# An LSTM step on Trainium2: the output gate in the bank of the other gates, and h Wh partly in 512 columns

## The chip, the cores and the metric

The kernel runs on one core of one Trainium2 chip. The metric is the device time of one launch in microseconds, as the median of three runs, and lower is better. The engines have the names of the profile: PE is TensorE (matrix products; PEld its weight loads), DVE is VectorE, ACT is ScalarE, POOL is GpSimd, SP issues transfers. Each runs its own instructions in order and waits for the others by semaphores. PSUM is the memory that TensorE writes its products to; this kernel uses all of its eight banks, each 512 fp32 columns wide.

## The reference

One LSTM layer over 512 steps, with a batch of 32 and 512 units, added to its input. Everything is fp32.

```python
xW = jnp.einsum('ntd,dg->ntg', x, Wx) + b
def step(carry, xw_t):
    prev_h, prev_c = carry
    a = xw_t + prev_h @ Wh
    i = sigmoid(a[:, :Hd]); f = sigmoid(a[:, Hd:2*Hd])
    o = sigmoid(a[:, 2*Hd:3*Hd]); g = tanh(a[:, 3*Hd:])
    next_c = f * prev_c + i * g
    next_h = o * tanh(next_c)
    return (next_h, next_c), next_h
out = x + swapaxes(scan(step, (h0, 0), swapaxes(xW, 0, 1)), 0, 1)
```

`prev_h @ Wh` needs the step before and so cannot be batched: it is 32 x 512 by 512 x 2048 in each step. `x @ Wx` needs no step and can be done ahead.

## The kernel before

**One step of the recurrence.** The gates lie in PSUM as 128 partitions by 512 columns: partition block j (32 partitions) holds the batch for units 128j to 128j+127, and the columns are four gates of 128 units, put in the order i, f, g, o by the host's layout of the weights. A step k is one call of `h_part` (L766), one `cell` (L797) and, between them, other work of TensorE, all written in the loop at L1065. `h_part` multiplies: for each of four row blocks k of Wh and each of four unit blocks j one matmul (L770) with a 32-column stationary block of h. The four j run side by side in four column strips of the array. In the profile an fp32 matmul is two records, so a step's 32 matmuls are 64 records.

**Two banks by turns, and where the output gate lies.** There are two gate banks, `gates[0]` and `gates[1]`. Step t has its gates i, f and g (columns 0 to 383, `IFG`) in `gates[t % 2]`, and its output gate (columns 384 to 511) in the other bank, `gates[(t + 1) % 2]`. So `h_part` runs sixteen matmuls of 384 columns into one bank, then sixteen of 128 columns into the other.

**Seeds.** Before TensorE adds h Wh, ScalarE copies the finished x Wx of that step into the bank: `seed_first(k + 2)` (L751, copy at L755) the first 384 columns of step k+2, `seed_last(k + 1)` (L757, copy at L761) the last 128 columns of step k+1, which lie in the same bank. Both stand in the program right behind the cell of step k. The matmuls accumulate onto the seed (`start=False`).

**The cell** (L797 to L817): on ScalarE the sigmoid of i and f (L807), the tanh of g (L808), the sigmoid of o (L809); on VectorE f c (L810), i g (L811), their sum c (L812); on ScalarE tanh c (L813); on VectorE the product with o (L814) and a transpose in 32 x 32 blocks (L815), which gives `ht`, the h that the next `h_part` loads as weights. GpSimd then adds x to h and SP stores it (L873, L876).

**The other work.** x Wx is computed some steps ahead by a fast scheme for matrix products that needs 26 block products in place of 32. Each of them is a job of seven products, and a product is four matmuls of 256 columns (L477). A job starts in its own window, the one of step k having the number v = k + 4, and its products are spread over the windows up to four later; `products(v)` (L486) issues those of a window behind `h_part`. From v = `START` on the jobs repeat with a cycle of `PER` = 32 windows, 26 jobs or 182 products to a cycle, so a window holds five or six. In the head, before `START`, a job sums over two factors and a window can hold up to fourteen. `evacuate(v)` (L495), which stands between `h_part` and `products`, moves the finished sums between PSUM and SBUF on ScalarE and VectorE, and `run_due` (L362) gives VectorE the sums for later jobs; all of these stand ahead of the cell in the two engines' queues. The results go to HBM and come back by `load_xw` on GpSimd's queue three steps ahead of their use.

**The end.** The last 40 steps use another form, `h_halves` (L779), which the change leaves as it is.

Of the kernel before, what the change touches and what calls it, by code (L numbers as in the profile page):

```python
# [14 lines left out]
P = 128  # L15
B = 32
T = 512
NJ = 4
G = 4
IFG = 3 * P  # L20
# [16 lines left out]
PER = ROW * MO  # L37
# [107 lines left out]
def windows_of(k):  # L145

    return [k + 4]


START = windows_of(HEAD - LEAD)[0]  # L150
# [4 lines left out]
def begin(n):  # L155

    half, at = divmod(n, R // 2)
    return PER // 2 * half + at + (at >= 5) + (at >= 9)
# [7 lines left out]
LAST = START + PER * (NSB - 1) + begin(R - 1)  # L166
HALVES = LAST + 3 - 4
# [14 lines left out]
def kernel(  # L182
# [9 lines left out]
    nc = tc.nc  # L192
# [11 lines left out]
    gates = [psum.tile([P, G * P], F32, name=f"gates_{i}") for i in range(2)]  # L204
# [13 lines left out]
    rows, xw, stored = {}, {}, {}  # L218
# [233 lines left out]
    jobs = {}  # L452
    count = 0

    def new_job(w, late5=False):
        nonlocal count
        job = Job()
        job.w, job.w5 = w, w + late5
        job.acc = accs[w % 2][:, w // 2 % 2]
        job.pp = pps[2 * count % 3], pps[(2 * count + 1) % 3]  # L460
        count += 1
        jobs[w] = job
        return job

    def product(job, s):
        dst = {
            1: job.acc,
            6: job.acc,
            7: job.acc,
            5: p5[:, 0],  # L470
            2: job.pp[0][:, 0],
            3: job.pp[0][:, 1],
            4: job.pp[1][:, 0],
        }[s]
        for m, (a, w) in enumerate(job.factors(s)):
            for t in range(4):
                nc.tensor.matmul(  # L477
                    dst[t * B : (t + 1) * B],
                    a[:, t],
                    w,  # L480
                    start=s in (1, 5) and m == 0,
                    stop=True,
                    skip_group_check=True,
                )

    def products(v):  # L486
        for late, ss in ((4, (4,)), (2, (7,)), (0, (1,)), (1, (6,)), (0, (5,)), (1, (5,)), (3, (2, 3))):
            job = jobs.get(v - late)
            for s in ss if job else ():
                if s != 5 or job.w5 == v:  # L490
                    product(job, s)
                if s == 4:
                    job.release()
# [207 lines left out]
    whole, given = [], [0, 0]  # L701
# [45 lines left out]
    def seed_half(t, m):  # L747
        if t < T:
            nc.scalar.copy(bank_half(m), half(xw[t], m))

    def seed_first(t):  # L751
        if t == HALVES:
            seed_half(t, 0)
        elif t < HALVES:
            nc.scalar.copy(gates[t % 2][:, 0:IFG], xw[t][:, 0:IFG])  # L755

    def seed_last(t):  # L757
        if t == HALVES:
            seed_half(t, 1)
        elif t < HALVES:  # L760
            nc.scalar.copy(gates[(t + 1) % 2][:, IFG:], xw[t][:, IFG:])  # L761

    state = {"c": c_init, "ht": h_init}
    ig = work.tile([P, P], F32, name="ig")

    def h_part(t):  # L766
        for g, cols in ((gates[t % 2], slice(0, IFG)), (gates[(t + 1) % 2], slice(IFG, G * P))):
            for k in range(NJ):
                for j in range(NJ):
                    nc.tensor.matmul(  # L770
                        g[j * B : (j + 1) * B, cols],
                        state["ht"][:, k, :],
                        wh_sb[:, k, j, cols],
                        start=False,
                        stop=True,
                        skip_group_check=True,
                    )
# [19 lines left out]
    def cell(t):  # L797
        n, tt = divmod(t, ROW)
        s = work.tile([P, G, P], F32, name=f"s_{t}", tag="s")
        fc = work.tile([P, P], F32, name=f"fc_{t}", tag="fc")  # L800
        c = work.tile([P, P], F32, name=f"c_{t}", tag="c", bufs=2)
        tc_t, h = ig, fc
        ht = work.tile([P, NJ, B], F32, name=f"ht_{t}", tag="ht", bufs=3)

        g = gates[t % 2].rearrange("p (g u) -> p g u", u=P)
        o = gates[(t + 1) % 2].rearrange("p (g u) -> p g u", u=P)[:, 3]
        nc.scalar.activation(s[:, 0:2], g[:, 0:2], AF.Sigmoid)  # L807
        nc.scalar.activation(s[:, 2], g[:, 2], AF.Tanh)  # L808
        nc.scalar.activation(s[:, 3], o, AF.Sigmoid)  # L809
        nc.vector.tensor_mul(fc, s[:, 1], state["c"])  # L810
        nc.vector.tensor_mul(ig, s[:, 0], s[:, 2])  # L811
        nc.vector.tensor_add(c, fc, ig)  # L812
        nc.scalar.activation(tc_t, c, AF.Tanh)  # L813
        nc.vector.tensor_mul(h, s[:, 3], tc_t)  # L814
        nc.vector.transpose(ht.rearrange("p q b -> p (q b)"), h)  # L815
        state["c"], state["ht"] = c, ht
        put_step(t)  # L817
# [50 lines left out]
    def put_step(t):  # L868
        n, tt = divmod(t, ROW)
        ht = state["ht"]  # L870
        if tt % 2 == 0:
            state["oc"] = opool.tile([P, 2, NJ, B], F32, name=f"oc_{t}", tag="oc")
        (nc.gpsimd if t < T - 3 else nc.vector).tensor_add(state["oc"][:, tt % 2], xr[t][:, tt % 2], ht)  # L873
        if tt % 2 == 1 or t == T - 2:
            m = tt % 2 + 1
            nc.sync.dma_start(  # L876
                out=out[n][:, (tt + 1 - m) * P : (tt + 1) * P],
                in_=state["oc"][:, 0:m].rearrange("p t q b -> p (t q b)"),
            )
# [3 lines left out]
    for u, (i, j) in zip(UNIT_AT, UNITS):  # L883
        job = new_job(u)
        job.kind = (i, j)
    for sb in range(NSB):
        for n in range(R):
            job = new_job(START + PER * sb + begin(n), n % (R // 2) in (4, 8, 12))
            job.kind = (sb, n)
    for w, j in zip(LATE_AT, LATE_ORDER):  # L890
        job = new_job(w)
# [125 lines left out]
    with tc.manual_schedule():  # L1017
# [23 lines left out]
        for op in prepare(0):  # L1041
            op()
        products(0)
        for t in range(1, 4):
            keep_direct(t, firsts[t])
# [4 lines left out]
        for v, t in enumerate(range(4, ROW), 1):  # L1050
            direct(t, gates[t % 2])
            for op in prepare(v):
                op()
            if v < 4:
                evacuate(v, 0)
            run_due(0, 2400 if v > 1 else 0)
            keep_direct(t, gates[t % 2])
            if v < 4:
                products(v)
                fetch(v)  # L1060
        seed_first(0)
        seed_last(0)
        seed_first(1)

        for k in range(T):  # L1065
            if k % 2 == 0 and k + 2 < T:
                load_residual(k + 2)
            if 2 * 4 - 3 <= k and k + 3 < LATE_END:
                load_xw(k + 3)
            (h_part if k < HALVES else h_halves)(k)  # L1070
            for m, v in enumerate(windows_of(k)):
                if v == START + 4:
                    assert len(due) == 0 or due[0][0] >= START
                    head_done()
                announce(v)
                room = HEAD_ROOM if v < START - 4 else ROOM if k < HALVES - 1 else HALF_ROOM
                run_due(v, room - evacuate(v, room))
                products(v)
                tail_products(v)
                fetch(v)  # L1080
                if k == T - 2:
                    x_last()
                if 2 * 4 - 4 <= k and k + 4 < LATE_END:
                    fill_bias(k + 4)
                if m == 0:
                    (cell if k < HALVES else cell_halves)(k)
                    seed_first(k + 2)
                    seed_last(k + 1)
                for op in prepare(v + 1):
                    op()  # L1090
# [52 lines left out]
```

## Time and profile before

| | us |
|---|---|
| median of three runs | 3089.14 (3089.09 to 3089.30) |
| the profiled execution | 3089.44 |
| its span, first to last instruction | 3087.6 |
| TensorE with a matmul in flight | 3077.6 |
| VectorE busy | 2247.7 |
| ScalarE busy | 1972.5 |

The page of the profile lists busy times by engine, the chain of work that ended last, and groups of instructions by source line; the timeline lists instructions by start time, with the idle time of the engine just before them and what ended it in brackets. A matmul's recorded duration includes its way through the array, so those of neighbours overlap; the distance from start to start is what a matmul costs in a stream.

### The profile page before, as it was taken

How to read it: one execution, taken by the hardware profiler on the slowest of the kernel's cores; microseconds unless marked ns; L12 is line 12 of the kernel's file. 1: busy time of each engine (PE TensorE's matmuls, PEld its weight loads, DVE VectorE, ACT ScalarE, POOL GpSimd, SP SyncE). 2: the span in 40 equal slices, each digit the busy share in tenths (PEclk: the TensorE clock that was granted, in tenths of full speed). 3: DMA queues.
4: the chain of work that ended last, by engine and by line, in shares of the span. 5: the costliest groups of instructions: out<-in, count | busy, mean ns of one | idle time of the engine just before them, and what ended most of it. 6: DMA issues, size and time to landing. Idle time of an engine off the chain costs nothing.

```text
span 3087.6 us, 133855 instructions
## 1 busy us (share of the span) xinstructions
PE 3077.6 (100%) x56756; PEld 2216.0 (72%) x56756; DVE 2247.7 (73%) x6345; ACT 1972.5 (64%) x5694; POOL 807.4 (26%) x1009
## 2 busy tenths in 40 slices
PE   9999999999999999999999999999999999999998
PEld 6777666666666666666666666677777777777766
DVE  6735777777777777777777777777777777777654
ACT  2556666666666666666666666766666666666654
POOL 0112222222222222222222222222222222222321
PEclk9999999999999999999999999999999999999999
DMA  8857898988989888898888988889898898887752
GB/s 281 260 149 191 222 261 216 261 226 225 260 216 254 223 241 238 216 265 217 253 228 217 265 221 250 225 220 261 216 260 224 227 255 222 253 229 222 188 114 45
DMA packets 345973, 696.14 MB, mean 225 GB/s; under 512 B 45216, under 2 KB 118176, under 8 KB 344864
## 3 DMA queue, kind: packets, MB, share of 16 engines
q1 hardware_dynamic: 273520, 557.27, 55.1%
q0 software_dynamic: 71424, 130.06, 26.8%
q8 instruction: 446, 7.31, 1.0%
q14 instruction: 151, 1.24, 0.1%
q10 hardware_dynamic: 432, 0.27, 0.0%
HBM read 503.65 MB, written 183.76 MB: 223 GB/s over the span
## 4 chain that ended last, share of the span: by engine, by line
PE 99%; DVE 1%; ACT 0%; DMA 0%; issue 0%; DVEq 0%
PE gates L770 53%; PE acc L477 17%; PE pp L477 17%; PE p L477 6%; PE gates L784 4%; PE gates L682 1%; PE pp L682 1%; PE acc L682 0%; PE pp L1021 0%; DMA xw<-t 0%; DVE fc L835 0%; DVE c L837 0%; DVE t L656 0%; DVE fc L841 0%; DVE ht L845 0%
## 5 line engine op out<-in xcount | busy, mean ns | idle before, releaser
L770 PE MATMUL gates<-wh_sb,ht 128*32 128x384 f32 (+1 forms) x30144 | 1759.3, 379 | 0.0
L770 PEld LDWEIGHTS gates<-wh_sb,ht 128*32 128x32 f32 x30144 | 1188.4, 110 | 551.9 <-issue 439.7
L873 POOL TENSOR_TENSOR oc<-xr,ht 128x128 f32<-128x128 f32 x509 | 385.5, 757 | 2243.1 <-DVE ht L815 2037.3
L732 POOL DMA_DIRECT2D xw<-xw x496 | 437.1, 881 | 20.4 <-issue 2.1
L807 ACT ACTIVATE s<-gates 128x256 f32<-128x256 f32 x472 | 182.0, 386 | 351.9 <-PE gates L770 341.6
L477 PE MATMUL pp<-wb,nodes 128*32 128x256 f32 x3808 | 342.4, 379 | 0.0
L728 ACT COPY xw<-bias_sb 128x512 f32<-128x512 f32 x496 | 314.0, 633 | 0.0
L810 DVE TENSOR_TENSOR fc<-s,c 128x128 f32<-128x128 f32 x471 | 136.6, 290 | 208.2 <-ACT s L807 205.2
L814 DVE TENSOR_TENSOR fc<-s,ig 128x128 f32<-128x128 f32 x472 | 137.9, 292 | 177.2 <-ACT ig L813 177.2
L516 ACT COPY pp<-pu 128x512 f32<-128x512 f32 x388 | 234.0, 603 | 50.2 <-DVE t L640 23.7
L518 DVE TENSOR_TENSOR pp<-acc,p 128x256 f32<-128x256 f32 x388 | 165.9, 427 | 137.1 <-ACT pp L517 137.1
L477 PE MATMUL pp<-wb,s 128*32 128x256 f32 x2576 | 231.2, 379 | 0.0
L477 PE MATMUL acc<-wa,s 128*32 128x256 f32 x2576 | 230.8, 379 | 0.0
L477 PE MATMUL acc<-wb,s 128*32 128x256 f32 x2576 | 230.7, 379 | 0.0
L477 PE MATMUL p<-wa,s 128*32 128x256 f32 x2576 | 230.6, 379 | 0.0
L809 ACT ACTIVATE s<-gates 128x128 f32<-128x128 f32 x472 | 131.1, 278 | 147.3 <-PE gates L770 147.3
L755 ACT COPY gates<-xw 128x384 f32<-128x384 f32 x468 | 221.2, 473 | 3.3 <-DVE nodes L698 3.0
L813 ACT ACTIVATE ig<-c 128x128 f32<-128x128 f32 x472 | 146.2, 310 | 101.5 <-DVE c L812 63.8
L511 DVE TENSOR_TENSOR pu<-acc,p 128x256 f32<-128x256 f32 x388 | 161.4, 416 | 46.0 <-ACT p L508 35.4
L517 ACT COPY pp<-acc 128x256 f32<-128x256 f32 x388 | 140.0, 361 | 83.0 <-DVE t L640 41.0
L477 PEld LDWEIGHTS pp<-wb,nodes 128*32 128x32 f32 x3808 | 167.4, 110 | 23.7
L815 DVE STREAM_TRANSPOSE ht<-fc 128x128 f32<-128x128 f32 x472 | 147.2, 312 | 50.3 <-DVE fc L814 1.4
(241 smaller groups left out, 4751.9 us busy)
## 6 DMA issues: line engine op xcount, KB each, us to landing
wb<-keep_b SPq DMA_DIRECT2D x322, 512.0 KB, 6.3
xw<-xw POOLq DMA_DIRECT2D x496, 256.0 KB, 5.6
wa<-keep_a SPq DMA_DIRECT2D x322, 384.0 KB, 5.2
xw<-t SPq DMA_DIRECT2D x408, 128.0 KB, 3.9
xw<-raw_sb SPq DMA_DIRECT2D x312, 128.0 KB, 4.0
xr<-in_x_dram SPq DMA_DIRECT2D x256, 128.0 KB, 5.5
out_dram<-oc SPq DMA_DIRECT2D x255, 128.0 KB, 4.4
row<-in_x_dram SPq DMA_DIRECT2D x63, 512.0 KB, 8.2
```

Source lines behind the costliest of these rows:

```text
L477: nc.tensor.matmul(dst[t * B : (t + 1) * B], a[:, t], w, start=s in (1, 5) and m == 0, stop=True, skip_group_check=True,)
L511: nc.vector.tensor_add(job.pu[:, 1], job.acc, job.p5)
L516: nc.scalar.copy(job.pp[0], job.pu)
L518: nc.vector.tensor_add(job.pp[1][:, 1], job.acc, job.p5)
L728: nc.scalar.copy(xw[t], bias_sb)
L732: nc.gpsimd.dma_start(out=xw[t], in_=stored[i][a], accum_op=mybir.AluOpType.add)
L755: nc.scalar.copy(gates[t % 2][:, 0:IFG], xw[t][:, 0:IFG])
L770: nc.tensor.matmul(g[j * B : (j + 1) * B, cols], state["ht"][:, k, :], wh_sb[:, k, j, cols], start=False, stop=True, skip_group_check=True,)
L807: nc.scalar.activation(s[:, 0:2], g[:, 0:2], AF.Sigmoid)
L813: nc.scalar.activation(tc_t, c, AF.Tanh)
L815: nc.vector.transpose(ht.rearrange("p q b -> p (q b)"), h)
L873: (nc.gpsimd if t < T - 3 else nc.vector).tensor_add(state["oc"][:, tt % 2], xr[t][:, tt % 2], ht)
```

## The change

The output gate of step t goes back to `gates[t % 2]`, beside i, f and g; `seed_first` copies all 512 columns at once and `seed_last` does nothing but for the last form. `h_part` multiplies its first `whole` row blocks of Wh in matmuls of 512 columns, and the other row blocks as before, first their 384 and then their 128 columns, all into the one bank. `whole` is three at 13 positions of the cycle of 32, two at three positions, one at one position, and none at the others. In the head it is four, that is all, in windows with more than seven products (`products_at` counts them) and none in the others. In the changed file the cell starts at L825 (L825, L826 and L827 are the three activations on ScalarE, L828 is the product f c on VectorE), the tanh of c is L831, the transpose L833, and the matmul of `h_part` is L788.

```diff
         elif t < HALVES:
-            nc.scalar.copy(gates[t % 2][:, 0:IFG], xw[t][:, 0:IFG])
+            nc.scalar.copy(gates[t % 2], xw[t])
...
         if t == HALVES:
             seed_half(t, 1)
-        elif t < HALVES:
-            nc.scalar.copy(gates[(t + 1) % 2][:, IFG:], xw[t][:, IFG:])
...
+    WIDE = {at: 3 for at in (0, 3, 10, 15, 16, 17, 19, 20, 21, 22, 26, 28, 31)} | {5: 2, 6: 1, 23: 2, 27: 2}
+
     def h_part(t):
-        for g, cols in ((gates[t % 2], slice(0, IFG)), (gates[(t + 1) % 2], slice(IFG, G * P))):
-            for k in range(NJ):
+        v = t + 4
+        if v < START:
+            whole = NJ if products_at(v) > 7 else 0
+        else:
+            whole = WIDE.get((v - START) % PER, 0) if v < LAST else 0
+        first, last = slice(0, IFG), slice(IFG, G * P)
+        parts = [(slice(0, G * P), range(whole))] + [(cols, range(whole, NJ)) for cols in (first, last)]
+        for cols, ks in parts:
+            for k in ks:
                 for j in range(NJ):
                     nc.tensor.matmul(
-                        g[j * B : (j + 1) * B, cols],
+                        gates[t % 2][j * B : (j + 1) * B, cols],
                         state["ht"][:, k, :],
                         wh_sb[:, k, j, cols],
                         start=False,
...
-        o = gates[(t + 1) % 2].rearrange("p (g u) -> p g u", u=P)[:, 3]
+        o = g[:, 3]
         nc.scalar.activation(s[:, 0:2], g[:, 0:2], AF.Sigmoid)
         nc.scalar.activation(s[:, 2], g[:, 2], AF.Tanh)
         nc.scalar.activation(s[:, 3], o, AF.Sigmoid)
```

```python
IN_ORDER = ((4, (4,)), (2, (7,)), (0, (1,)), (1, (6,)), (0, (5,)), (1, (5,)), (3, (2, 3)))

def products_at(v):
    found = 0
    for late, ss in IN_ORDER:
        job = jobs.get(v - late)
        for s in ss if job else ():
            if s != 5 or job.w5 == v:
                found += 1 if job.w >= START else 2
    return found
```

More of the change, by code (lines that the diff above doesn't have):

```diff
@@ L484, in product @@
                 )
+    IN_ORDER = ((4, (4,)), (2, (7,)), (0, (1,)), (1, (6,)), (0, (5,)), (1, (5,)), (3, (2, 3)))
+    def products_at(v):
+        found = 0
+        for late, ss in IN_ORDER:
+            job = jobs.get(v - late)
+            for s in ss if job else ():
+                if s != 5 or job.w5 == v:
+                    found += 1 if job.w >= START else 2
+        return found
     def products(v):
-        for late, ss in ((4, (4,)), (2, (7,)), (0, (1,)), (1, (6,)), (0, (5,)), (1, (5,)), (3, (2, 3))):
+        for late, ss in IN_ORDER:
             job = jobs.get(v - late)
```

## The prediction

> **What bounds the kernel now.** I read the page first, then the waits of TensorE, then the timeline of a few steps in the middle of the run. The page says that TensorE sets the end:
>
> ```profile
> span 3087.6 us, 133855 instructions
> PE 3077.6 (100%) x56756; PEld 2216.0 (72%) x56756; DVE 2247.7 (73%) x6345; ACT 1972.5 (64%) x5694; POOL 807.4 (26%) x1009
> ...
> PE 99%; DVE 1%; ACT 0%; DMA 0%; issue 0%; DVEq 0%
> ```
>
> Only 10 us of the span are without a matmul, and the view of the waits has TensorE waiting for another engine six times in all:
>
> ```profile
> PE gates L784 <- DVE fc L835: 4.0, 5, 1.2
> PE pp L1021 <- DVE c_init L249: 1.1, 1, 1.1
> ```
>
> None of them is in the 472 steps of L770, so today the recurrence is hidden in every step. How closely it is hidden is read from the timeline. Three steps in a row, TensorE alone (a row is start, time to its last modelled end, line; eight records of L477 are one product of the other work):
>
> ```profile
> 615.06 3.67 PE L770 MATMUL gates<-wh_sb,ht 128*32 128x384 f32 x64
> ...
> 621.11 3.67 PE L770 MATMUL gates<-wh_sb,ht 128*32 128x384 f32 x64
> 624.56 0.65 PE L477 MATMUL pp<-wb,row 128*32 128x256 f32 x8
> 624.99 0.65 PE L477 MATMUL acc<-wb,s 128*32 128x256 f32 x8
> ...
> 626.72 3.67 PE L770 MATMUL gates<-wh_sb,ht 128*32 128x384 f32 x64
> ```
>
> A step is h Wh (3.45 us, 621.11 to 624.56) and then products of 0.43 us each (624.56 to 624.99). The step at 615.06 has six products and takes 6.05 us; the one at 621.11 has five and takes 5.61. Beside them runs the cell of the same step, here for the step that begins at 626.72 (call that moment H0) and ends at 632.76, 6.04 us later:
>
> ```profile
> 629.60 0.38 ACT L807 ACTIVATE s<-gates 128x256 f32<-128x256 f32 x1 [0.89 <-PE gates L770]
> 629.88 0.27 ACT L808 ACTIVATE s<-gates 128x128 f32<-128x128 f32 x1
> 630.02 0.29 DVE L810 TENSOR_TENSOR fc<-s,c 128x128 f32<-128x128 f32 x1 [0.27 <-ACT s L807]
> ...
> 630.48 0.28 ACT L809 ACTIVATE s<-gates 128x128 f32<-128x128 f32 x1 [0.32 <-PE gates L770]
> 630.55 0.29 DVE L812 TENSOR_TENSOR c<-fc,ig 128x128 f32<-128x128 f32 x1
> ...
> 630.87 0.31 ACT L813 ACTIVATE ig<-c 128x128 f32<-128x128 f32 x1
> ...
> 631.09 0.47 ACT L755 COPY gates<-xw 128x384 f32<-128x384 f32 x1
> 631.21 0.29 DVE L814 TENSOR_TENSOR fc<-s,ig 128x128 f32<-128x128 f32 x1 [0.38 <-ACT ig L813]
> ...
> 631.59 0.27 ACT L761 COPY gates<-xw 128x128 f32<-128x128 f32 x1
> 631.61 0.31 DVE L815 STREAM_TRANSPOSE ht<-fc 128x128 f32<-128x128 f32 x1
> ...
> 632.76 0.87 PE L770 MATMUL gates<-wh_sb,ht 128*32 128x384 f32 x8
> ```
>
> Three times matter. The first sigmoid (L807) starts 2.88 us after H0, when the sixteen 384-column matmuls are through. The output gate's sigmoid (L809) starts 3.76 us after H0, when the sixteen 128-column ones are through. From L807 to the end of the transpose (631.92) the cell takes 2.32 us, and L809 is not on that path: its result is first wanted by L814. So h stands ready 0.84 us before TensorE wants it in a six-product step, and 0.43 us less than that in a five-product step. The present order lives on one overlap: 0.88 us of the cell run while TensorE still writes the output gate into the other bank.
>
> **The change part by part.**
>
> *Output gate into the same bank.* In the changed program's instruction order the first sigmoid (L825) waits for TensorE and the output gate's (L827) has no wait of its own; before, L807 and L809 each had one. TensorE's semaphore is now raised once per step, at the last matmul of h Wh, by all its 20 or 32 at a time, where it was raised by 16 and again by 16. So the first sigmoid can start only when the output gate's columns are done too, that is when L809 starts today: 3.76 us after H0. The split into 384 and 128 columns that remains in the code then frees nothing early. From there the cell needs its 2.32 us (the output sigmoid now follows L826 at once and is ready some 0.8 us into the cell, before the tanh of c has even begun at 1.27). Then h goes to TensorE. That hand-over is seen as a real wait only at the end of the run:
>
> ```profile
> 3068.99 0.24 DVE L845 STREAM_TRANSPOSE ht<-fc 128x64 f32<-128x64 f32 x1
> ...
> 3069.38 1.50 PE L784 MATMUL gates<-wh_sb,ht 128*32 128x256 f32 x24 [1.17 <-DVE fc L835]
> ```
>
> It is 0.15 us from the transpose's end (3069.23). From above it is bounded by the tightest kind of step that does not stall, where the next block began 0.27 us after the transpose ended:
>
> ```profile
> 696.93 0.31 DVE L815 STREAM_TRANSPOSE ht<-fc 128x128 f32<-128x128 f32 x1
> ...
> 697.51 3.67 PE L770 MATMUL gates<-wh_sb,ht 128*32 128x384 f32 x64
> ```
>
> I take 0.15, since there TensorE truly waited, for the same kind of tile. A step can then be no shorter than S = 3.76 + 2.32 + 0.15 = 6.23 us (6.35 with the upper bound), whatever its products: TensorE ends its six products at 6.04, its five at 5.61, and waits. Of the 472 steps 311 have six products and 139 five, counted in the program's order; 22, all at the start, have seven or more (7 x 0.43 + 3.45 = 6.46) and stay hidden. The added stall is 311 x 0.19 = 59.1 us and 139 x 0.62 = 86.2 us.
>
> The Trainium skill, "PSUM — Partial Sum Buffer", section "PSUM bank collisions raise a hardware error", says that TensorE writing and ScalarE reading one bank in the same 32 partitions at once is an error even at different columns, so a semaphore has to guard the whole bank. By that rule the wait of L825 for the last matmul is not an accident of the build, and the sum is the one above; by the rows alone, in which L807 runs beside L770, one could count on keeping the overlap, and the sum would be that of the second rival. No run here shows a collision.
>
> *Merged columns.* What a merged block saves is bounded by a block that is in 512 columns already, the direct x Wx of the first rows:
>
> ```profile
> 22.03 3.65 PE L682 MATMUL gates<-raw_sb,row 128*32 128x512 f32 x32
> ```
>
> That is eight groups of four records in 3.65 us, against 3.67 for the eight of 384 and eight of 128: 0.02 us in eight groups, 2.5 ns for each group merged. Three row blocks are six groups (15 ns). The program merges three blocks in 179 stalled steps, two in 42, one in 14 (1270 groups), and 148 groups in hidden steps of the start: 1418 x 2.5 ns = 3.5 us in all.
>
> *Seeds.* L755 and L761 (0.47 and 0.27) become one copy of 512 columns. The nearest row of that size into a bank is
>
> ```profile
> L516 ACT COPY pp<-pu 128x512 f32<-128x512 f32 x388 | 234.0, 603 | 50.2 <-DVE t L640 23.7
> ```
>
> 0.60 us, so ScalarE saves 0.14 us per step. It stands behind the tanh of the cell and seeds a step that is two further on; the cover is the whole next step, and I cost it at nothing.
>
> *Behind the later wait.* On ScalarE the seed and the next step's evacuation copies queue behind L825. The seed would end 3.76 + 1.49 (L755 after L807) + 0.60 = 5.85 us after H0, 0.38 before the next block; the copies then wait for TensorE anyway, as in this row, which starts 0.31 us after the block at 632.76:
>
> ```profile
> 633.07 0.59 ACT L628 COPY raw_sb<-pp 128x512 f32<-128x512 f32 x1 [1.20 <-PE pp L477]
> ```
>
> On VectorE the next sums start 0.15 us before the next block and not 0.84. There the cover is thinner: it is the first rival.
>
> *Sum.* 59.1 + 86.2 - 3.5 = +141.8 us. On the span: 3087.6 + 141.8 = 3229.4; around it lie 1.8 us (profiled execution 3089.44), and the median of the runs is 0.3 lower, 3089.14. That gives 3231.
>
> **The rivals.**
>
> *VectorE falls behind.* In some steps VectorE is not ready when the first sigmoid is:
>
> ```profile
> DVE fc L810 <- ACT s L807: 205.2, 270, 5.2
> ...
> 618.78 0.29 DVE L810 TENSOR_TENSOR fc<-s,c 128x128 f32<-128x128 f32 x1
> ...
> 1013.15 0.43 DVE L518 TENSOR_TENSOR pp<-acc,p 128x256 f32<-128x256 f32 x1 [1.57 <-ACT pp L517]
> ```
>
> L810 waits for ScalarE in 270 of 471 steps; in the step of 615.06 it starts 3.72 us after H0 where the clean step has 3.30. In the changed kernel it is wanted at 3.76 + 0.42 = 4.18, so 0.46 is to spare. If all of VectorE's work moved by the 0.69 that it starts later, it would be 0.23 late, and 201 such steps cost 46 us more: 3277. Against it: this lateness comes from work like L518, which sits waiting (1.57 us) for a copy that waits for TensorE, and so keeps its distance to H0. It decides from 4.18 us after H0.
>
> *The first gates are released by their columns.* If L825 were freed by the last 384-column matmul, the overlap stays. With three blocks merged those matmuls end six groups of about 0.11 us later, 0.64, inside the 0.84 of the six-product steps, and the other steps keep their order. Then only the merging is left: 3089.1 - 3.5 = 3085.6, 0.11% less, not told from no change. For it: the profile has L807 and L809 released separately. Against it: the changed program has a single wait and a single raise, at the end of the block. It decides at where L825 starts, 3.5 or 3.74 us after H0 in a merged step and 2.88 or 3.76 in an unmerged one.
>
> **How the numbers follow.** I give the forecast 0.87, VectorE behind 0.07, release by columns 0.03, and 0.03 to something else. For the forecast alone, each row that is read to 0.01 us can move 450 steps by 4.5 us either way, some 15 us for the few that make up S and the steps' lengths, and a hand-over of 0.27 would add 54 us. Below, nothing shortens a chain whose parts are all measured, so the range goes 16 us down, and up by a little over half of the 54: 3215 to 3262. It leaves out the two rivals' own values and little of the forecast. A measurement of this kernel tells 0.2% (6.2 us) from no change. Slower by more than that: forecast, VectorE and most of the rest, 0.96; within it, 0.03; faster, 0.01.
>
> **What would show it.** After the change the waits of TensorE should have a new row, the h block waiting for VectorE's transpose, some 450 times and about 145 us in all; L825 should start about 3.75 us after the block's first matmul in every step, L827 should show no wait for TensorE; steps of five and six products should be of one length, 6.21 to 6.23 us. TensorE's busy time should hardly change. L825 starting 2.9 us after H0 would make the first part wrong; steps of 6.4 us with L828 (the new place of L810) not waiting for the sigmoid would speak for VectorE; a hand-over above 0.2 us would make the price too small.

## The result and the profile after

The changed kernel takes 3173.77 us (3173.62 to 3173.95) against 3089.16: slower by 84.6 us, ratio 1.0274 with a 95% interval of 1.0261 to 1.0287. That it would be slower was forecast; the loss of 141.8 us was too large, and 3173.8 lies below the range that began at 3215.

The page of the changed kernel:

```profile
span 3172.1 us, 121564 instructions
PE 3121.8 (98%) x51084; PEld 1583.7 (50%) x51084; DVE 2244.1 (71%) x6345; ACT 1830.3 (58%) x5222; POOL 807.1 (25%) x1009
...
PE 88%; DVE 7%; ACT 3%; issue 1%; DMA 0%; DVEq 0%
```

The last row is the chain that ended last, by engine: it was 99% TensorE and now runs through VectorE and ScalarE for a tenth of the time. The work of TensorE did not grow (fewer, wider records), yet its busy time rose by 44 us. A matmul's recorded time includes its way through the array: eight records of L477 last 0.61 us while the next eight start after 0.43, so the beginning of each wait still counts as busy. For the same reason the view of the waits shows only a part of the stall at the matmuls: in a step of six products the last record ends after the next block has begun (644.02 + 0.61 = 644.63 against 644.49 in the rows below), and no wait is left to see. The weight loads, which read h, tell the number of waits:

```profile
PEld gates L788 <- DVE ht L833: 212.1, 450, 0.8
...
PE gates L788 <- DVE ht L833: 40.0, 142, 0.3
```

450 waits for the transpose is the forecast number of stalled steps, 311 + 139. The timeline of TensorE, two block starts in a row (the step from 626.19 has six products, the one from 632.29 five; the second row shows only the beginning of its block):

```profile
626.19 3.66 PE L788 MATMUL gates<-wh_sb,ht 128*32 128x384 f32 x64
632.29 2.14 PE L788 MATMUL gates<-wh_sb,ht 128*32 128x384 f32 x24
```

and the next block, at 638.40, with its whole cell (all engines, some rows left out):

```profile
638.03 0.31 DVE L833 STREAM_TRANSPOSE ht<-fc 128x128 f32<-128x128 f32 x1
...
638.40 0.16 PEld L788 LDWEIGHTS gates<-wh_sb,ht 128*32 128x32 f32 x8 [0.77 <-DVE ht L833]
638.40 3.65 PE L788 MATMUL gates<-wh_sb,ht 128*32 128x512 f32 x40 [0.29 <-DVE ht L833]
...
642.11 0.38 ACT L825 ACTIVATE s<-gates 128x256 f32<-128x256 f32 x1 [1.65 <-PE gates L788]
...
642.39 0.27 ACT L826 ACTIVATE s<-gates 128x128 f32<-128x128 f32 x1
...
642.53 0.29 DVE L828 TENSOR_TENSOR fc<-s,c 128x128 f32<-128x128 f32 x1 [1.00 <-ACT s L825]
642.55 0.28 ACT L827 ACTIVATE s<-gates 128x128 f32<-128x128 f32 x1
...
643.38 0.31 ACT L831 ACTIVATE ig<-c 128x128 f32<-128x128 f32 x1 [0.55 <-DVE c L830]
...
643.59 0.61 PE L477 MATMUL pp<-wb,row 128*32 128x256 f32 x8
643.60 0.58 ACT L766 COPY gates<-xw 128x512 f32<-128x512 f32 x1
643.72 0.29 DVE L832 TENSOR_TENSOR fc<-s,ig 128x128 f32<-128x128 f32 x1 [0.38 <-ACT ig L831]
...
644.02 0.61 PE L477 MATMUL pp<-wb,s 128*32 128x256 f32 x8
644.12 0.31 DVE L833 STREAM_TRANSPOSE ht<-fc 128x128 f32<-128x128 f32 x1
...
644.49 0.85 PE L788 MATMUL gates<-wh_sb,ht 128*32 128x384 f32 x8
```

The steps from 626.19, 632.29 and 638.40 take 6.10, 6.11 and 6.09 us, whether they have six products or five (the one from 638.40 has six). L825 starts 3.71 us after the block (this one has three merged row blocks; 3.73 without), and L827 follows L826 without a wait for TensorE: the first gates are released with the last. The cell is 2.32 us from 642.11 to 644.43, as before. It is above all the last link that is not as forecast: h is ready at 644.43 and the next block starts at 644.49, 0.06 us later and not 0.15.

### The profile page after: what moved, and what is told of

Its sections match the earlier page's. It is cut to its first block, busy times and chain, and to the rows that moved or that the text cites. A ratio compares the mean times of both kernels' runs of the same rounds, so it can differ in the third digit from the quotient of the medians.

```text
span 3172.1 us, 121564 instructions
## 1 busy us (share of the span) xinstructions
PE 3121.8 (98%) x51084; PEld 1583.7 (50%) x51084; DVE 2244.1 (71%) x6345; ACT 1830.3 (58%) x5222; POOL 807.1 (25%) x1009
## 4 chain that ended last, share of the span: by engine, by line
PE 88%; DVE 7%; ACT 3%; issue 1%; DMA 0%; DVEq 0%
PE gates L788 53%; PE pp L477 14%; PE acc L477 11%; PE p L477 4%; PE gates L802 4%; ACT s L825 2%; DVE ht L833 1%; ACT ig L831 1%; DVE fc L832 1%; DVE c L830 1%; DVE fc L828 1%; DVE ig L829 1%; PE gates L693 1%; PE pp L693 1%; PE acc L693 0%
## 5 line engine op out<-in xcount | busy, mean ns | idle before, releaser
L788 PE MATMUL gates<-wh_sb,ht 128*32 128x384 f32 (+2 forms) x24504 | 1720.3, 430 | 40.0 <-DVE ht L833 40.0
L788 PEld LDWEIGHTS gates<-wh_sb,ht 128*32 128x32 f32 x24504 | 720.0, 110 | 1082.0 <-issue 866.2
L825 ACT ACTIVATE s<-gates 128x256 f32<-128x256 f32 x472 | 181.4, 384 | 706.8 <-PE gates L788 706.8
L828 DVE TENSOR_TENSOR fc<-s,c 128x128 f32<-128x128 f32 x471 | 137.8, 292 | 465.1 <-ACT s L825 465.1
L831 ACT ACTIVATE ig<-c 128x128 f32<-128x128 f32 x472 | 145.9, 309 | 259.6 <-DVE c L830 259.6
L477 PE MATMUL pp<-wb,nodes 128*32 128x256 f32 x3808 | 292.7, 379 | 0.0
L766 ACT COPY gates<-xw 128x512 f32<-128x512 f32 x468 | 271.1, 579 | 11.2 <-DVE nodes L709 11.0
L477 PE MATMUL pp<-wb,s 128*32 128x256 f32 x2576 | 198.0, 379 | 0.0
L477 PE MATMUL acc<-wa,s 128*32 128x256 f32 x2576 | 198.0, 379 | 0.0
L477 PE MATMUL p<-wa,s 128*32 128x256 f32 x2576 | 198.0, 379 | 0.0
L477 PE MATMUL acc<-wb,s 128*32 128x256 f32 x2576 | 198.0, 379 | 0.0
L833 DVE STREAM_TRANSPOSE ht<-fc 128x128 f32<-128x128 f32 x472 | 146.9, 311 | 50.3 <-DVE fc L832 1.4
L515 ACT COPY pu<-acc 128x256 f32<-128x256 f32 x388 | 143.9, 371 | 25.9 <-PE acc L477 25.9
L802 PE MATMUL gates<-wh_sb,ht 128*32 128x256 f32 x2560 | 146.4, 380 | 4.0 <-DVE fc L853 4.0
```

The costliest lines, as they stand in the source:

```text
L477: nc.tensor.matmul(dst[t * B : (t + 1) * B], a[:, t], w, start=s in (1, 5) and m == 0, stop=True, skip_group_check=True,)
L766: nc.scalar.copy(gates[t % 2], xw[t])
L788: nc.tensor.matmul(gates[t % 2][j * B : (j + 1) * B, cols], state["ht"][:, k, :], wh_sb[:, k, j, cols], start=False, stop=True, skip_group ...
L802: nc.tensor.matmul(bank_half(m)[j * B : (j + 1) * B], state["ht"][:, k, :], half(wh_sb[:, k, j], m), start=False, stop=True, skip_group_ch ...
```

## The experiments

**Sharing the bank without merging.** The changed kernel with no row block in 512 columns:

```diff
-        if v < START:
-            whole = NJ if products_at(v) > 7 else 0
-        else:
-            whole = WIDE.get((v - START) % PER, 0) if v < LAST else 0
+        whole = 0
```

> The changed kernel with no row block in 512 columns: the output gate in the bank of the others, and all h Wh in 384 and then 128 columns. Theory (the whole loss is the cell that starts after the last matmul of the block; merging is worth 2.4 ns for each of 1418 groups): 3173.8 + 3.4 = about 3177 us, every step of five or six products 6.10 us, hand-over from the transpose to TensorE 0.055 us as in the changed kernel. Rival (merging itself lengthens the block or delays the first sigmoid, and costs part of the 85 us): clearly below 3173.8, by up to 30 us.

3176.79 us (ratio to the kernel before 1.0284, interval 1.0268 to 1.0299). That is 3.0 us more than the changed kernel: merging is worth 3.0 us there, not a cost, and the bank carries the whole loss, 87.6 us. TensorE's waits hardly differ:

```profile
PE gates L785 <- DVE ht L830: 39.8, 142, 0.3
```

**All row blocks merged.** The same lines replaced by `whole = NJ`.

> The changed kernel with all four row blocks in 512 columns in every step. Theory (nothing is released before the end of the block, so the 384 and 128 columns that are left free nothing early): 2330 more groups merged in stalled steps at 2.4 ns, 3173.8 - 5.6 = about 3168 us, stalled steps 6.08 us. Rival (the 128 columns at the end do free the first gates early in part of the steps): slower than 3173.8, by up to 0.2 us for each of some 270 steps with fewer than three merged blocks, up to 3230 us.

3167.87 us (1.0254, 1.0239 to 1.0270), 5.9 us less than the changed kernel where 5.6 were expected. So keeping 384 and 128 columns apart only costs here: with the gates in one bank, nothing is freed before the end of the block.

**A second wait at the hand-over.** The changed kernel with the seed in two copies, of which the short one is made late, so that TensorE's first matmul waits for ScalarE too:

```diff
         elif t < HALVES:
-            nc.scalar.copy(gates[t % 2], xw[t])
+            nc.scalar.copy(gates[t % 2][:, 0:IFG], xw[t][:, 0:IFG])
...
         if t == HALVES:
             seed_half(t, 1)
+        elif t < HALVES:
+            nc.scalar.copy(gates[t % 2][:, IFG:], xw[t][:, IFG:])
...
-                    seed_first(k + 2)
                     seed_last(k + 1)
+                    seed_first(k + 2)
```

> The changed kernel with the seed in two copies again, the 128 columns of step k+1 right after the tanh of step k and the 384 of step k+2 after them. Both end before the transpose does, but TensorE's first matmul of a block now waits for two engines, and the second wait is an instruction of its own (51 ns in the profile before). Theory (the 0.15 us that the prediction read at the end of the run held such a wait instruction, and the changed kernel has none): the hand-over is about 0.145 us and not 0.055, the first sigmoid starts 3.73 to 3.76 us after the block's start, stalled steps 6.19 to 6.22 us, 3214 to 3228 us. Rival (the hand-over at the end of the run is longer for its half-size transpose or its other form, and a second wait that is long over costs nothing): 3174 to 3178 us, hand-over 0.055.

3209.74 us (1.0390, 1.0375 to 1.0406), 36.0 us more than the changed kernel: the theory by its hand-over, 4 us under its lower end. Its timeline around one hand-over:

```profile
643.28 0.26 ACT L772 COPY gates<-xw 128x128 f32<-128x128 f32 x1
...
643.81 0.31 DVE L835 STREAM_TRANSPOSE ht<-fc 128x128 f32<-128x128 f32 x1
...
644.24 0.19 PEld L790 LDWEIGHTS gates<-wh_sb,ht 128*32 128x32 f32 x8 [0.82 <-ACT gates L766]
644.27 1.06 PE L790 MATMUL gates<-wh_sb,ht 128*32 128x512 f32 x8 [0.36 <-DVE ht L835]
```

The copy that TensorE also waits for (L772; the row names the copy after it as releaser) ended at 643.54, long before h was ready at 644.12. The first matmul still comes 0.15 us after h and not 0.06. What differs is counted in the view of the matmul's line, the kernel before, the changed one and this one in turn (operation, count, least, median and longest ns):

```profile
L770 PEldq EVENT_SEMAPHORE  x473: 51/51/51, 44.5 to 2877.4; - x158
```

```profile
L788 PEldq EVENT_SEMAPHORE  x1: 51/51/51, 44.1 to 44.1; - x1
```

```profile
L790 PEldq EVENT_SEMAPHORE  x473: 51/51/51, 44.4 to 2998.8; - x158
```

The second wait is an instruction of TensorE's sequencer, once per step, and it stands between h and the weight loads: in this run's trace it starts 0.04 us after the transpose has ended, and takes 0.051. The kernel before has it in every step too, but there TensorE still has products to work on; at the end of that kernel's run, where the prediction read its 0.15 us, TensorE is idle. The matmuls of that last form (L784) have it once in each of their 40 steps:

```profile
L784 PEldq EVENT_SEMAPHORE  x40: 51/51/51, 2883.7 to 3079.0; - x40
```

36 us over 450 steps are 0.08 us per step; the hand-over grew by 0.09, and the first sigmoid of this kernel starts about 0.01 earlier in the step.

**The output gate first, no bank shared.** The kernel before with its two parts exchanged:

```diff
-        for g, cols in ((gates[t % 2], slice(0, IFG)), (gates[(t + 1) % 2], slice(IFG, G * P))):
+        for g, cols in ((gates[(t + 1) % 2], slice(IFG, G * P)), (gates[t % 2], slice(0, IFG))):
```

> The kernel before with the two parts of h Wh exchanged: the output gate's sixteen matmuls of 128 columns first, into the other bank as before, then the sixteen of 384 columns. No bank is shared and nothing is merged. Theory (the loss is the lost overlap of 0.88 us, wherever the output gate lies): the first sigmoid starts 3.76 us after the block's start; with the second wait of that kernel the hand-over is 0.145 us, so steps of five and six products are 6.22 us long and the time is about 3229 us. Rival (the loss comes from sharing one bank between TensorE and ScalarE): 3089 us, as before.

3215.68 us (1.0409, 1.0392 to 1.0427), 126.5 us more than before, with the gates in two banks. One step of it, L809 being the output gate's sigmoid:

```profile
708.59 3.66 PE L770 MATMUL gates<-wh_sb,ht 128*32 128x128 f32 x64
712.31 0.39 ACT L807 ACTIVATE s<-gates 128x256 f32<-128x256 f32 x1 [2.34 <-PE gates L770]
...
714.32 0.31 DVE L815 STREAM_TRANSPOSE ht<-fc 128x128 f32<-128x128 f32 x1
...
714.78 3.66 PE L770 MATMUL gates<-wh_sb,ht 128*32 128x128 f32 x64 [0.36 <-DVE ht L815]
```

The first sigmoid starts 3.72 us after the block, h follows 2.32 later, the hand-over with its second wait is 0.15, and the step is 6.19 us long. So the loss belongs to the overlap: a cell that begins at the end of the block is late wherever the output gate lies. Sharing the bank is only what makes it begin there, through the one wait that the changed program has for the whole bank. This run was 13 us under its expectation, which had the first sigmoid at 3.76.

## Why the prediction was wrong

*The mechanism was right.* The wait of L825 for the whole block, the 450 stalled steps, steps of one length for five and six products, the unchanged cell of 2.32 us, and the output sigmoid off the path all came as written. The first run shows that sharing the bank alone costs 87.6 us; the last one, that losing the overlap without sharing a bank costs 126.5 us, of which the run with the second wait puts some 36 down to that wait.

*The term that failed was the hand-over in S = 3.76 + 2.32 + 0.15.* It measured 0.06 us. The prediction took it from the end of the run "since there TensorE truly waited, for the same kind of tile". The wait was real (the row names L835, but in the program's instruction order the wait is for the transpose), but that matmul waits for two engines, and the new block for one: in the changed program VectorE's semaphore is the only one that the first matmul still needs. The instruction order that showed the single wait of L825 showed this too. The bounds, 0.15 to 0.27, both came from matmuls with a second wait, so the true value lay below both; nothing in the rows excluded a shorter one, and the prediction's sentence that nothing shortens the chain was where it went wrong. 0.09 us in 450 steps are 41 us, most of the 57 between forecast and result; the second-wait run puts 36 of them back.

The upper bound was misread too: 0.27 us is not the tightest step of the kernel before. Of its 145 steps of five or six products that begin after 2021 us, 23 have between 0.14 and 0.22 us from the transpose's end to the first matmul of the next block. In this one it is 0.14 (2588.24 to 2588.38), while other column strips still work on a product:

```profile
2587.93 0.31 DVE L815 STREAM_TRANSPOSE ht<-fc 128x128 f32<-128x128 f32 x1
...
2588.38 0.48 PE L770 MATMUL gates<-wh_sb,ht 128*32 128x384 f32 x1
2588.39 0.39 PE L477 MATMUL pp<-wb,s 128*32 128x256 f32 x2
```

*The start of the first sigmoid was read 0.03 too late.* 3.73 in the changed kernel against L809's 3.76 before, some 14 us over the 450 steps. The weight loads show one difference: four of them take 0.17 us in the block before and 0.13 in the changed one, that is, the four column strips are started closer together.

```profile
627.04 0.17 PEld L770 LDWEIGHTS gates<-wh_sb,ht 128*32 128x32 f32 x4 [0.15 <-issue]
```

```profile
638.85 0.13 PEld L788 LDWEIGHTS gates<-wh_sb,ht 128*32 128x32 f32 x4 [0.30 <-issue]
```

Whether that spread is the cause was not tried by itself, and the second-wait run speaks against it as the whole answer: its loads take 0.16 and its first sigmoid is as early. The cause of these 0.03 us stays open.

*Merging was sized right.* 2.5 ns for each group of four records gave 3.5 us for the change; taking it out cost 3.0, and carrying it through gained 5.9 for 5.6 expected.

*The rivals.* VectorE did not fall behind: L828 waits for L825 in 468 of 471 steps (1.00 us in the timeline above), and the cell is 2.32 us. The release by columns did not happen: L825 starts 3.71 us after the start of a merged block, not 3.5, and 3.73 without merging, not 2.88. The Trainium skill ("PSUM — Partial Sum Buffer", section "PSUM bank collisions raise a hardware error") asks for a semaphore that guards the bank and not the address. The changed programs have such a wait and these runs show no collision; no run left the wait out, so the rule itself was not tested.

*The waits to look for.* 450 waits came, but as 212 us at the weight loads and 40 at the matmuls, and TensorE's busy time did change, for the reason told with the page. The length of the steps was the sound measure.

## What to carry to other kernels

Splitting an output over two banks can be worth far more than the matmuls it costs: here 0.88 us of a 2.32 us cell ran under the rest of the block, for 2.5 ns per extra group. Before a change puts two things into one bank, ask which reader is released when. When a latency is taken from another place of the same trace, compare the waits of the two instructions: a wait for two engines is another link than a wait for one.

## What the runs showed that was not expected

A second wait on TensorE, for something long done, costs 0.09 us at a hand-over that is on the path (0.06 us with one wait, 0.15 with two, of which the wait instruction itself is 0.051). With such a wait in every step the kernel before shows no wait of TensorE for h: in its five- and six-product steps h was ready 0.27 to 0.84 us early up to 2021 us, and never less than 0.14 us early after that.
